# Latent attention's output turned on VectorE in 32 by 32 squares, and the range test summed on GpSimd

## The chip, the cores and the metric

The kernel runs on one core of a Trainium2 chip. The metric is the device time of one execution in microseconds (us); shown are the median of three runs and, for the reading of the profile, one profiled execution. The engines are TensorE (PE, with its weight loads PEld), VectorE (DVE), ScalarE (ACT), GpSimd (POOL) and SyncE (SP), which here only issues DMAs.

## The reference, cut to what matters

Eight sequences of 1024 tokens and 256 channels, all in fp32, go through two layers with a residual each: first a causal latent attention, then a stack of two local-attention layers, which the change does not touch. The first, on normalised x:

```
c_kv   = x @ W_kv_down                        # 256 -> 128
k_rope = rotary(c_kv @ W_k_rope)              # 32 channels, shared by the heads
k, v   = c_kv @ W_k_up, c_kv @ W_v_up         # 16 heads of 16
q      = x @ W_q                              # 16 heads of 16
q_rope = rotary(x @ W_q_rope)
scores = (q k^T per head + q_rope k_rope^T) / sqrt(48), causal
attn   = softmax(scores) @ v
out    = x + attn @ W_o
```

The part `q_rope k_rope^T` is the same for all 16 heads, so the kernel takes its exponential once for all heads and multiplies: exp(a + b) = exp(a) exp(b).

## The kernel before, in words

The latent attention (`mla`) works through the batches b = 0 to 7, each in 36 steps. A step is a unit of the score matrix: four heads (group g, heads 4g to 4g+3) by 128 keys (block kb) by up to 512 queries (half c; c = 1, the later queries, comes first). Units 0 to 25 are c = 1, 26 to 35 are c = 0. The scores are held with the keys on the partitions.

The order on PE, DVE, ACT and POOL is written out by hand; each engine runs its own queue in order. At step s:

- `scores` (L422, L430): PE makes the scores of unit s into two PSUM tiles `sc`, ACT takes the exponentials into two tiles `pt` of 128 by 1024.
- `turned` (L444): DVE multiplies both `pt` of unit s-1 by the rotary exponentials `er`, which lie in SBUF as `pt` does.
- `values` (L455): PE multiplies the `pt` of unit s-2 by the values into `acc`, which has 32 rows for each of the four heads: 16 of output, then a row of ones' products, the softmax's denominator (VW = 17 columns for each head in `v`). When a group of heads is complete for a half, ACT copies `acc` to `oaT` (512 columns, queries along the free axis).
- then the tasks that a table puts beside the step (`at(step, who, name, ...)`, who = -1, 0, 1, 2 being the batch before, this one and the next two), and one finished group.

The tasks that matter here:

- `rotary` (L400, L401, L403): PE makes one block `psR` of the rotary scores in a PSUM bank, ACT takes the exponential into `er` and adds each row up in `most` (an accumulator, which is a read instruction of its own on ACT), DVE takes the row's minimum into `least`, and POOL clears the triangle above the diagonal in the blocks that have one. The eight blocks of c = 1 are made at steps 27 to 34 for the next batch, the four of c = 0 at steps 11 to 15 for the batch itself; for batch 0 the blocks of c = 1 are made in a row before step 0. `most` and `least` are tested at the end against TURN = 1e17 and 1/TURN; their verdict decides with others whether an exact path, not run here, has to replace the result.
- `value` (L76): v = c_kv @ W_v_up, copied from PSUM by DVE.
- `finished`: four transpositions on PE (`flip`, L203) turn a group's `oaT` to 128 queries by four heads in PSUM (`pst`); DVE takes the reciprocal of the denominators (L472, `rs`) and multiplies (L473) into `onat`.
- `out_turn` (L203, L78): for two blocks of 128 queries, four more transpositions on PE turn `onat` back to channels by queries (`pso`), and ACT copies them to `oT`.
- `out_add` (L200, L500, L501): PE multiplies `oT` by `wout` (W_o), DVE adds x, and SP stores the result to DRAM (`x2d`).

PSUM banks for these tasks come from a pool of two (`bank`, L203's and L200's outputs alike). A matrix product with weights (`times`) is cut in four instructions of 32 output rows each. In the last batch the tail's tasks are held back and run after the last step; the local layers follow, their weights being loaded meanwhile.

Of the kernel before, what the change touches and what calls it, by code (L numbers as in the profile page):

```python
# [29 lines left out]
F32 = mybir.dt.float32  # L30
AF = mybir.ActivationFunctionType
ALU = mybir.AluOpType
# [49 lines left out]
def preln_mla_local_kernel(  # L82
# [72 lines left out]
    def mla(ctx: ExitStack, verdict):  # L155
# [42 lines left out]
        def times(out, w, rhs, start, stop):  # L198
            for four in QUARTER:
                nc.tensor.matmul(out[four], w[:, four], rhs, start=start, stop=stop)  # L200

        def flip(out, t):
            nc.tensor.transpose(out, t, ident)  # L203
# [13 lines left out]
        nc.sync.dma_start(wknat, W_k_up)  # L217
        wv = wp.tile([P, D], F32, name="wv")
        nc.sync.dma_start(wv, W_v_up)
        wout = late.tile([P, 2, D], F32, name="wout")  # L220
        nc.sync.dma_start(wout, W_o.rearrange("(c p) d -> p c d", p=P))

# [34 lines left out]

        ers = [late.tile([P, 1280 + 2048 * c], F32, name=f"er{c}") for c in range(2)]  # L260

        most = wp.tile([P, B * 12], F32, name="most")
        least = wp.tile([P, B * 12], F32, name="least")

        class Batch:

# [128 lines left out]
            def rotary(self, c, kb):  # L395
                q0, w, er = self.block(c, kb)
                ps = bank(f"psR{self.b}_{c}_{kb}")
                times(ps[:, :w], self.rk[:, kb * P : (kb + 1) * P], self.rq[:, q0 : q0 + w], True, True)
                n = 12 * self.b + 8 * (1 - c) + kb
                nc.scalar.activation(er, ps[:, :w], AF.Exp, scale=SCALE, accum_out=most[:, n : n + 1])  # L400
                nc.vector.tensor_reduce(least[:, n : n + 1], er, AX.X, ALU.min)  # L401
                if q0 == kb * P:
                    nc.gpsimd.affine_select(  # L403
                        out=er[:, :P], in_=er[:, :P], pattern=[[1, P]],
                        compare_op=ALU.is_ge, fill=0.0, base=0, channel_multiplier=-1,
                    )

            def start(self):
                b = self.b
                self.onat = late.tile([P, NT, NH, HD], F32, tag="onat", name=f"onat{b}")  # L410
                self.rs = small.tile([P, NT, NH], F32, tag="rs", name=f"rs{b}")
                self.acc = {}

            def scores(self, key, parts):

# [49 lines left out]
                return ended  # L465

            def finished(self, c, g, oT):
                ps = bank(f"pst{self.b}_{c}_{g}").rearrange("p (i h d) -> p i h d", i=4, h=4)
                for i in range(4):
                    flip(ps[:, i].rearrange("p h d -> p (h d)"), oT[:, i * P : (i + 1) * P])  # L470
                r = self.rs[:, 4 * c : 4 * c + 4, 4 * g : 4 * g + 4]
                nc.vector.reciprocal(r, ps[:, :, :, HD])  # L472
                nc.vector.tensor_tensor(  # L473
                    self.onat[:, 4 * c : 4 * c + 4, 4 * g : 4 * g + 4, :], ps[:, :, :, :HD],
                    r.unsqueeze(3).to_broadcast([P, 4, 4, HD]), ALU.mult,
                )

            def out_turn(self, t):
                if t == 4:
                    self.oTs, self.adds = {}, {}  # L480
                elif t == 0:
                    verdict(self.rs.rearrange("p t h -> p (t h)"), f"a{self.b}")
                ps = bank(f"pso{self.b}_{t}").rearrange("p (i q) -> p i q", i=4)
                for i in range(4):
                    flat = self.onat[:, t + i // 2].rearrange("p h d -> p (h d)")
                    flip(ps[:, i, :], flat[:, (i % 2) * P : (i % 2 + 1) * P])
                self.oTs[t] = late.tile([P, 4, P], F32, tag="oT", name=f"oT{self.b}_{t}", bufs=2)
                on_a(self.oTs[t], ps)

            def out_add(self, t, i, c=None):  # L490

                if i == 0 and not c:
                    self.adds[t] = bank(f"psx{self.b}_{t}").rearrange("p (i d) -> p i d", i=2)
                ps = self.adds[t]
                for n in range(2) if c is None else (c,):
                    times(ps[:, i], self.oTs[t][:, 2 * i + n, :], wout[:, n, :], n == 0, n == 1)
                if i == 1 and c != 0:
                    del self.oTs[t], self.adds[t]
# [11 lines left out]
        for step, who, *what in (  # L510
# [5 lines left out]
            (5, 0, "query", 0, 0, 1), (5, -1, "out_turn", 0), (5, 1, "normalise", 0, 1),  # L516
            (6, -1, "out_add", 0, 0), (6, -1, "out_turn", 2), (6, 1, "normalise", 1, 0),
# [23 lines left out]
            (30, 1, "rotary", 1, 3), (30, 0, "out_turn", 4),  # L541
# [3 lines left out]
            (34, 1, "rotary", 1, 5), (34, 0, "out_turn", 6), (34, 2, "statistics", 1, 0),  # L545
            (35, 0, "out_add", 6, 0), (35, 0, "out_add", 6, 1, 0),
        ):
            at(step, who, *what)
# [28 lines left out]
        line, done = [], []  # L577
        with tc.manual_schedule(engines={E.PE, E.DVE, E.Activation, E.Pool}):
            for b in range(B + 1):
                for step in range(len(units) if b < B else 9):  # L580
                    if b == B - 1 and step == ALONE:
                        banks.close()
                        third = banks.enter_context(tc.tile_pool(name="pscore2", bufs=1, space=PSUM))
                        shared = itertools.cycle((pscore, pscore, third))
                    if b < B:
                        if step == 0:
                            batches[b].start()
                        line.append((batches[b], units[step], batches[b].scores(step, units[step])))
                    if len(line) > 1 or b == B:
                        for bt, unit, pts in line[-2 : -1] if b < B else line[-1:] if step == 0 else []:  # L590
                            bt.turned(unit, pts)
                    if b == B and step == 0:
                        for act, args in held[:3]:
                            act(*args)
                    ended = []
                    if len(line) > 2 or b == B and line:
                        bt, unit, pts = line.pop(0)
                        ended = [(bt, e) for e in bt.values(unit, pts)]
                    if b == B and step == 0:
                        for act, args in held[3:]:  # L600
                            act(*args)
                    do(b, step)
                    if done:
                        bt, e = done.pop(0)
                        bt.finished(*e)
                    done += ended

        ok = small.tile([P, 2, B * 12], F32, tag="okr", name="okr", bufs=1)
        nc.vector.tensor_scalar(ok[:, 0, :], most, TURN, None, ALU.is_le)
        nc.vector.tensor_scalar(ok[:, 1, :], least, 1 / TURN, None, ALU.is_ge)  # L610
        verdict.add(ok.rearrange("p m n -> p (m n)"), "turn")


    ST = CH // P
# [1155 lines left out]
```

## Time and profile before

| | |
|---|---|
| median of 3 runs | 3413.71 us (3412.76 to 3415.95) |
| profiled execution | 3414.97 us, span 3413.2 us |
| latent attention | up to about 1030 us of the span |
| from one batch's stores of x2d to the next's | 123.02 us |
| PE, DVE, ACT, POOL busy in one such period (274.00 to 397.02 us) | 122.0, 108.2, 91.8, 9.7 us |
| granted PE clock in it | 1.00 |

How to read the profile's groups: line, engine, operation, output and inputs with their shapes, the number of instructions, then busy us and the mean ns of one, then the engine's idle time just before them and what ended it. Instructions of one engine overlap a little at their ends, so the distance from start to start is somewhat shorter than the mean duration (for two L444 in a row 2.27 us, for one 1.22). In a timeline a row has the start, the length of a run of instructions from first start to last end, and their number. POOL's spans are rough.

### The profile page before, as it was taken

What the parts mean: (1) busy time and instruction counts of PE and PEld (TensorE: products, weight loads), DVE (VectorE), ACT (ScalarE), POOL (GpSimd) and SP (SyncE); (2) the same over time, 40 slices, a digit from 0 to 9 for tenths busy, and PEclk for the clock granted to TensorE, in tenths of its full rate; (3) what the DMA queues carried; (4) which work ended last, traced back from release to release, by engine and by line L of the source; (5) the groups of instructions that cost most, each with busy time, mean ns of one, the idle gap of its engine ahead of it and who ended that gap; (6) DMA issues with size and microseconds to landing.
All of it is one profiled execution on the core that took longest, in us unless ns stands there. A gap on an engine that the chain in (4) does not pass through costs nothing.

```text
span 3413.2 us, 80002 instructions
## 1 busy us (share of the span) xinstructions
PE 3344.6 (98%) x34690; PEld 1847.4 (54%) x34690; DVE 2585.4 (76%) x3785; ACT 1702.7 (50%) x2106; POOL 1344.3 (39%) x1031
## 2 busy tenths in 40 slices
PE   8999999999997899999999999999999999999999
PEld 2434333443434565666566666566666666666665
DVE  6888988988887777777767776667777767777763
ACT  5777777777762344444444344444344444344441
POOL 1000000000006655555555555555555555545540
PEclk9999999999999999999999999999999999999999
DMA  1000000000032333233232333334243233333231
GB/s 62 8 20 26 8 20 26 11 20 11 14 110 83 86 87 94 78 106 88 78 99 82 90 95 106 99 96 118 83 118 94 85 108 86 102 108 91 82 94 45
DMA packets 203575, 248.82 MB, mean 73 GB/s; under 512 B 23455, under 2 KB 171342, under 8 KB 203086
## 3 DMA queue, kind: packets, MB, share of 16 engines
q1 hardware_dynamic: 201230, 241.21, 24.3%
q8 instruction: 274, 4.49, 0.6%
q10 hardware_dynamic: 1984, 2.41, 0.2%
q14 instruction: 87, 0.71, 0.1%
HBM read 134.50 MB, written 109.05 MB: 71 GB/s over the span
## 4 chain that ended last, share of the span: by engine, by line
PE 87%; DVE 7%; ACT 2%; issue 2%; POOL 1%; DMA 1%; SPq 0%; ACTq 0%; DVEq 0%
PE ag L1024 16%; PE pair L824 12%; PE sc L422 9%; PE acc L455 8%; PE psy L1059 7%; PE psw L969 7%; PE pv L851 6%; PE o L936 5%; PE pair L895 4%; PE psR L200 2%; PE psq L200 2%; PE psx L200 2%; PE s L944 1%; DVE turned L863 1%; DVE rs L948 1%
## 5 line engine op out<-in xcount | busy, mean ns | idle before, releaser
L444 DVE TENSOR_TENSOR pt<-pt,er 128x1024 f32<-128x1024 f32 x576 | 676.6, 1223 | 6.7 <-ACT pt L430 5.6
L430 ACT ACTIVATE pt<-sc 128x1024 f32<-128x1024 f32 x576 | 559.4, 1024 | 231.5 <-PE sc L422 209.4
L1024 PE MATMUL ag<-d,l 128*128 128x512 f32 x1408 | 640.6, 597 | 1.3 <-ACT ge L1032 0.8
L838 POOL TENSOR_TENSOR t<-t,t 128x1024 f32<-128x1024 f32 x128 | 301.9, 2358 | 756.0 <-DVE t L834 756.0
L824 PE MATMUL pair<-l_qkv,xT 128*128 128x512 f32 x1024 | 469.1, 601 | 3.0 <-ACT pt L901 1.0
L1024 PEld LDWEIGHTS ag<-d,l 128*128 128x128 f32 x1408 | 262.2, 190 | 310.0 <-issue 276.7
L901 ACT ACT_TABLE_LOAD x120 | 154.0, 1283 | 547.8 <-PE pair L895 547.7
L125 POOL TENSOR_TENSOR rn<-ss,half 128x16 f32<-128x16 f32 x128 | 372.9, 2913 | 13.8
L422 PE MATMUL sc<-q,k 32*128 32x512 f32 (+3 forms) x3072 | 347.7, 524 | 4.7 <-ACT pt L430 4.6
L831 DVE TENSOR_TENSOR t<-pair,l_cos 128x1024 f32<-128x1024 f32 x128 | 156.4, 1222 | 245.8 <-ACT sq L829 241.1
L824 PEld LDWEIGHTS pair<-l_qkv,xT 128*128 128x128 f32 x1024 | 190.5, 192 | 238.4 <-issue 207.1
L455 PE MATMUL acc<-pt,v 128*32 128x512 f32 (+3 forms) x3072 | 316.2, 498 | 0.1
L829 ACT ACTIVATE sq<-pair 128x1024 f32<-128x1024 f32 x128 | 131.1, 1024 | 303.4 <-issue 234.4
L1059 PE MATMUL psy<-l,hid 128*128 128x256 f32 x1280 | 281.5, 379 | 0.0
L1033 DVE SCALAR_TENSOR_TENSOR hid<-ag,l_b,ge 128x512 f32<-128x512 f32 x160 | 116.0, 725 | 206.8 <-ACT ge L1032 178.9
L1059 PEld LDWEIGHTS psy<-l,hid 128*128 128x128 f32 x1280 | 243.2, 190 | 46.7 <-issue 15.3
L901 ACT ACTIVATE pt<-pair 128x1024 f32<-128x1024 f32 (+1 forms) x256 | 235.0, 968 | 57.7 <-PE pair L895 56.4
L403 POOL TENSOR_SCALAR_AFFINE_SELECT er<-er 128x128 f32<-128x128 f32 x64 | 47.2, 737 | 530.0 <-DVE least L401 530.0
L844 POOL TENSOR_TENSOR t<-t,rn 128x1024 f32<-128x1024 f32 x128 | 243.4, 1902 | 10.0
L936 PEld LDWEIGHTS o<-pt,v 128*32 128x32 f32 x7680 | 201.4, 110 | 77.5 <-issue 70.8
L936 PE MATMUL o<-pt,v 128*32 128x128 f32 x7680 | 237.4, 274 | 3.4 <-POOL pt L903 3.2
L851 PE MATMUL pv<-l_qkv,xT 128*128 128x512 f32 x512 | 240.6, 592 | 0.0
(131 smaller groups left out, 4851.3 us busy)
## 6 DMA issues: line engine op xcount, KB each, us to landing
z<-turned SPq DMA_DIRECT2D x512, 128.0 KB
qkT<-z SPq DMA_DIRECT2D x128, 512.0 KB
y<-xs SPq DMA_DIRECT2D x128, 128.0 KB
h<-y SPq DMA_DIRECT2D x32, 512.0 KB
x<-in_L_attn_x_dram SPq DMA_DIRECT2D x16, 512.0 KB
x2d<-x SPq DMA_DIRECT2D x32, 256.0 KB
xs<-x2d SPq DMA_DIRECT2D x16, 512.0 KB
x<-x2d SPq DMA_DIRECT2D x16, 512.0 KB
```

The lines of the kernel that those rows point to most:

```text
L125: nc.gpsimd.tensor_tensor(out_, in_, half[:, :n], ALU.pow)
L422: nc.tensor.matmul(two[n // 2][:, n % 2, lo : lo + w], self.k[g][rows, kb * P : (kb + 1) * P], self.q[rows, g // 2, q0 : q0 + w], start=Tr ...
L430: nc.scalar.activation(pt, sc, AF.Exp, scale=SCALE)
L444: nc.vector.tensor_tensor(t, t, er.to_broadcast([P, 1024 // w, w]), ALU.mult)
L455: nc.tensor.matmul(self.acc[g][32 * n : 32 * n + 32, q0 - c * 512 :], self.v[:, kb, h * VW : h * VW + 32], pts[n // 2][:, n % 2, lo : lo + w],
L824: nc.tensor.matmul(qk[:, n].rearrange("p h d -> p (h d)"), self.left(i)[c], w["qkv"][:, c, n * INNER : (n + 1) * INNER], start=(c == 0), s ...
L838: nc.gpsimd.tensor_tensor(t1, t1, t2, ALU.add)
L851: nc.tensor.matmul(pv, self.left(i)[c], self.w["qkv"][:, c, 2 * INNER :], start=(c == 0), stop=(c == 1))
L901: nc.scalar.activation(pt[:, :, : n * P], flat[:, :, : n * P], AF.Exp, scale=-1.0)
L936: nc.tensor.matmul(o[32 * j : 32 * j + 32, g, a, :], vs[m][:, h * DH + a * 32 : h * DH + a * 32 + 32], pts[m][g][:, place(j), off : off + ...
L1024: nc.tensor.matmul(ps, w["1"][:, c, i, :], d[:, c, :], start=(c == 0), stop=(c == 1))
L1059: nc.tensor.matmul(ps[:, t, :], hid[:, i, cols], w["2"][:, i, :], start=(t == i == 0), stop=False)
```

## The change

- `finished` no longer uses PE. DVE transposes `oaT` itself, which it does within squares of 32 by 32: each head's 32 rows by 512 queries become 16 squares with 32 queries on the partitions (`nat`). Reciprocal and product follow, now from SBUF; the results of two groups (e = 0, 1) lie side by side in one tile, so that its squares are 32 wide.
- `out_turn` goes. In its place `turn_back`, one step after the second group of a pair is finished, transposes that tile once more on DVE, which gives `oT` directly: 512 queries, and the channels of eight heads on the partitions, in another order than before (head 4 (2m + e) + r has partitions 32 r + 16 e and on). The rows of `wout` are loaded in the same order, by eight DMAs instead of one.
- The copy of v from PSUM moves from DVE to ACT.
- The range test: no row sums and no minima. ACT takes a second exponential of each rotary block, with the sign reversed (`inverse`, one buffer of 128 by 512), and POOL adds both `er` and `inverse` into one tile of running sums (`ends`). At the end its maximum is compared with TURN. POOL's clearing of the triangle comes after the adds.

```diff
-        nc.sync.dma_start(wout, W_o.rearrange("(c p) d -> p c d", p=P))
+        for e in range(2):
+            for r in range(4):
+                lo = 32 * r + HD * e
+                nc.sync.dma_start(
+                    wout[lo : lo + HD],
+                    W_o.rearrange("(m e r p) d -> e r p m d", m=2, e=2, r=4)[e, r],
+                )
...
-                on_v(
+                on_a(
                     self.v[:, 2 * g : 2 * g + 2, : NH * VW].rearrange("p a (h d) -> p a h d", h=NH)[..., :HD],
...
-                nc.scalar.activation(er, ps[:, :w], AF.Exp, scale=SCALE, accum_out=most[:, n : n + 1])
-                nc.vector.tensor_reduce(least[:, n : n + 1], er, AX.X, ALU.min)
+                nc.scalar.activation(er, ps[:, :w], AF.Exp, scale=SCALE)
+                inverse = wp.tile([P, 512], F32, tag="inverse", name=f"inverse{self.b}_{c}_{kb}")
+                nc.scalar.activation(inverse[:, :w], ps[:, :w], AF.Exp, scale=-SCALE)
+                for what in (er, inverse[:, :w]):
+                    nc.gpsimd.tensor_tensor(ends[:, :w], ends[:, :w], what, ALU.add)
...
             def finished(self, c, g, oT):
-                ps = bank(f"pst{self.b}_{c}_{g}").rearrange("p (i h d) -> p i h d", i=4, h=4)
-                for i in range(4):
-                    flip(ps[:, i].rearrange("p h d -> p (h d)"), oT[:, i * P : (i + 1) * P])
...
+                nat = late.tile([P, 16, 32], F32, tag="onat", name=f"onat{self.b}_{c}_{g}", bufs=3)
+                nc.vector.transpose(nat.rearrange("p b d -> p (b d)"), oT)
+                r = self.rs[:, c, g]
+                nc.vector.reciprocal(r, nat[:, :, HD])
+                e = g % 2
+                if e == 0:
+                    self.onat[c, g // 2] = nat
                 nc.vector.tensor_tensor(
...
+                    self.onat[c, g // 2][:, :, HD * e : HD * e + HD], nat[:, :, :HD],
+                    r.unsqueeze(2).to_broadcast([P, 16, HD]), ALU.mult,
+                )
+
+            def turn_back(self, c, g):
+                if g % 2:
+                    t = late.tile([P, 512], F32, tag="oT", name=f"oT{self.b}_{c}_{g}", bufs=3)
+                    nc.vector.transpose(t, self.onat.pop((c, g // 2)).rearrange("p b d -> p (b d)"))
+                    self.oTs[c, g // 2] = t
...
+        nc.vector.tensor_reduce(ok, ends, AX.X, ALU.max)
+        nc.vector.tensor_scalar(ok, ok, TURN, None, ALU.is_le)
```

In the table of tasks the four `out_turn` entries go and nothing else moves; in the main loop `turn_back` stands before `finished`, one step behind it.

More of the change, by code (lines that the diff above doesn't have):

```diff
@@ L260, in mla @@
         ers = [late.tile([P, 1280 + 2048 * c], F32, name=f"er{c}") for c in range(2)]
-        most = wp.tile([P, B * 12], F32, name="most")
-        least = wp.tile([P, B * 12], F32, name="least")
+        ends = wp.tile([P, 512], F32, name="ends")
+        nc.gpsimd.memset(ends, 0.0)
         class Batch:
@@ L398, in rotary @@
                 times(ps[:, :w], self.rk[:, kb * P : (kb + 1) * P], self.rq[:, q0 : q0 + w], True, True)
-                n = 12 * self.b + 8 * (1 - c) + kb
-                nc.scalar.activation(er, ps[:, :w], AF.Exp, scale=SCALE, accum_out=most[:, n : n + 1])
-                nc.vector.tensor_reduce(least[:, n : n + 1], er, AX.X, ALU.min)
+                nc.scalar.activation(er, ps[:, :w], AF.Exp, scale=SCALE)
[3 more added lines that the diff above has]
+                    nc.gpsimd.tensor_tensor(ends[:, :w], ends[:, :w], what, ALU.add)
                 if q0 == kb * P:
@@ L409, in start @@
                 b = self.b
-                self.onat = late.tile([P, NT, NH, HD], F32, tag="onat", name=f"onat{b}")
-                self.rs = small.tile([P, NT, NH], F32, tag="rs", name=f"rs{b}")
-                self.acc = {}
+                self.rs = small.tile([P, 2, 4, 16], F32, tag="rs", name=f"rs{b}")
+                self.acc, self.onat, self.oTs, self.adds = {}, {}, {}, {}
             def scores(self, key, parts):
@@ L467, in finished @@
             def finished(self, c, g, oT):
-                ps = bank(f"pst{self.b}_{c}_{g}").rearrange("p (i h d) -> p i h d", i=4, h=4)
-                for i in range(4):
-                    flip(ps[:, i].rearrange("p h d -> p (h d)"), oT[:, i * P : (i + 1) * P])
-                r = self.rs[:, 4 * c : 4 * c + 4, 4 * g : 4 * g + 4]
-                nc.vector.reciprocal(r, ps[:, :, :, HD])
+                nat = late.tile([P, 16, 32], F32, tag="onat", name=f"onat{self.b}_{c}_{g}", bufs=3)
[5 more added lines that the diff above has]
+                    self.onat[c, g // 2] = nat
                 nc.vector.tensor_tensor(
-                    self.onat[:, 4 * c : 4 * c + 4, 4 * g : 4 * g + 4, :], ps[:, :, :, :HD],
-                    r.unsqueeze(3).to_broadcast([P, 4, 4, HD]), ALU.mult,
-                )
[L478 to L488, printed above, removed]
+                    self.onat[c, g // 2][:, :, HD * e : HD * e + HD], nat[:, :, :HD],
+                    r.unsqueeze(2).to_broadcast([P, 16, HD]), ALU.mult,
+                )
+            def turn_back(self, c, g):
[3 more added lines that the diff above has]
+                    self.oTs[c, g // 2] = t
+                if (c, g) == (0, 3):
+                    verdict(self.rs.rearrange("p c g b -> p (c g b)"), f"a{self.b}")
             def out_add(self, t, i, c=None):
@@ L495, in out_add @@
                 for n in range(2) if c is None else (c,):
-                    times(ps[:, i], self.oTs[t][:, 2 * i + n, :], wout[:, n, :], n == 0, n == 1)
+                    col = (t + i) % 4 * P
+                    times(ps[:, i], self.oTs[t // 4, n][:, col : col + P], wout[:, n, :], n == 0, n == 1)
                 if i == 1 and c != 0:
-                    del self.oTs[t], self.adds[t]
+                    del self.adds[t]
                     two = slice(t, t + 2)
@@ L515, in mla @@
             (4, 0, "keys", 1, 1, 1), (4, 0, "query", 0, 0, 0), (4, 1, "normalise", 0, 0),
-            (5, 0, "query", 0, 0, 1), (5, -1, "out_turn", 0), (5, 1, "normalise", 0, 1),
-            (6, -1, "out_add", 0, 0), (6, -1, "out_turn", 2), (6, 1, "normalise", 1, 0),
+            (5, 0, "query", 0, 0, 1), (5, 1, "normalise", 0, 1),
+            (6, -1, "out_add", 0, 0), (6, 1, "normalise", 1, 0),
             (7, -1, "out_add", 0, 1), (7, -1, "out_add", 2, 0, 0),
@@ L540, in mla @@
             (29, 1, "rotary", 1, 2), (29, 1, "rotary", 1, 7),
-            (30, 1, "rotary", 1, 3), (30, 0, "out_turn", 4),
+            (30, 1, "rotary", 1, 3),
             (31, 1, "rotary", 1, 6), (31, 0, "out_add", 4, 0),
@@ L544, in mla @@
             (33, 1, "rotary", 1, 4),
-            (34, 1, "rotary", 1, 5), (34, 0, "out_turn", 6), (34, 2, "statistics", 1, 0),
+            (34, 1, "rotary", 1, 5), (34, 2, "statistics", 1, 0),
             (35, 0, "out_add", 6, 0), (35, 0, "out_add", 6, 1, 0),
@@ L576, in mla @@
         E = mybir.EngineType
-        line, done = [], []
+        line, done, turning = [], [], []
         with tc.manual_schedule(engines={E.PE, E.DVE, E.Activation, E.Pool}):
@@ L592, in mla @@
                     if b == B and step == 0:
-                        for act, args in held[:3]:
+                        for act, args in held[:2]:
                             act(*args)
@@ L599, in mla @@
                     if b == B and step == 0:
-                        for act, args in held[3:]:
+                        for act, args in held[2:]:
                             act(*args)
                     do(b, step)
+                    if turning:
+                        bt, e = turning.pop(0)
+                        bt.turn_back(*e)
                     if done:
@@ L605, in mla @@
                         bt.finished(*e)
+                        turning.append((bt, e[:2]))
                     done += ended
[L608 to L611, printed above, removed]
+        ok = small.tile([P, 1], F32, tag="okr", name="okr", bufs=1)
+        nc.vector.tensor_reduce(ok, ends, AX.X, ALU.max)
+        nc.vector.tensor_scalar(ok, ok, TURN, None, ALU.is_le)
+        verdict.add(ok, "turn")
     ST = CH // P
```

## The prediction

> **What bounds the kernel now.** First the page: busy shares, then the chain.
>
> ```profile
> PE 3344.6 (98%) x34690; PEld 1847.4 (54%) x34690; DVE 2585.4 (76%) x3785; ACT 1702.7 (50%) x2106; POOL 1344.3 (39%) x1031
> ...
> PE 87%; DVE 7%; ACT 2%; issue 2%; POOL 1%; DMA 1%; SPq 0%; ACTq 0%; DVEq 0%
> ```
>
> TensorE carries 87% of the chain. The change touches only the latent attention, about the first 1030 us, so next the engines in one of its periods: the stores of x2d start at 150.98, 274.00 and 397.02 us, so a batch takes 123.02 us.
>
> ```profile
> 274.00:397.02 123.02, 122.01 (x1352) 49.37 (x1348) 108.24 (x142) 91.79 (x126) 9.70 (x10) 1.00 0.06 19
> ```
>
> The columns are PE, PEld, DVE, ACT and POOL, busy us (and instructions). PE is the bound at 122.0 of 123.0; DVE has 14.8 us left per batch, ACT 31, POOL nearly all. Then the groups by form, for what is taken from PE and DVE:
>
> ```profile
> L203 PE MATMUL pst<-ident,oaT 128*128 128x128 f32 x256 | 42.0, 287 | 3.5 <-ACT er L400 3.4 <-ACT oaT L78 0.2
> ...
> L203 PE MATMUL pso<-ident,onat 128*128 128x128 f32 x128 | 21.1, 286 | 0.7 <-DVE onat L473 0.7
> ...
> L863 DVE STREAM_TRANSPOSE turned<-t 128x512 f32<-128x512 f32 x28 | 18.1, 682 | 4.0 <-POOL t L844 4.0
> ```
>
> Last the timelines of DVE and POOL where both work, because the change gives POOL much to do:
>
> ```profile
> 387.79 2.44 DVE L444 TENSOR_TENSOR pt<-pt,er 128x1024 f32<-128x1024 f32 x2
> ...
> 387.94 1.21 POOL L403 TENSOR_SCALAR_AFFINE_SELECT er<-er 128x128 f32<-128x128 f32 x1 [9.43 <-DVE least L401]
> ```
>
> ```profile
> 2476.80 1.96 DVE L1077 TENSOR_TENSOR x<-xs,x 128x512 f32<-128x512 f32 x1
> ...
> 2476.31 1.90 POOL L844 TENSOR_TENSOR t<-t,rn 128x1024 f32<-128x1024 f32 x1
> ```
>
> The select normally takes 0.29 us; begun inside a product `pt*er`, it takes 1.21, ending just after the first of the two products. The other way round, L1077 (0.69 us alone) was begun inside a POOL product and took 1.96: it ended 0.55 us after POOL did. The two engines exclude each other, a whole instruction at a time.
>
> [...] the trace's nearest row (L838, 1024 columns) is 2358 ns, 2.30 ns a column[...]
>
> **The change part by part.**
>
> *PE, removed.* 64 `pst` and 32 `pso` sets of four flips. In the PE timeline the next matmul starts 0.585 us after a set starts (276.36 to 276.95), so 96 x 0.585 = 56.2 us. At step 15 the second set waits 0.48 us for a PSUM bank; with it gone, 8 x 0.48 = 3.8. Together **-60 us**: a batch asks PE for 115.5 us.
>
> *DVE.* Out: the 96 minima, 48 x 0.682 + 16 x (0.550 + 0.418 + 0.278) = 52.7, and 32 copies of v at 0.692 = 22.1. In: 96 transpositions like L863 at 0.682 = 65.5. Reciprocal and product by rs are as many as before (249, 424 ns; now from SBUF, not shown, taken alike; the width is the same, so either way under 0.1 us each). Net -9 us, 108.2 to 107.0 a batch. By itself this hides behind PE: adding DVE's work less PE's over the steps, DVE falls at most 3.7 us behind (step 3, where a finished group, turn_back and statistics meet). It may be some 4 us late: the values of a step are asked for two steps later, about 7.5 us after its scores start, and are ready at the earliest after 3.5.
>
> *ACT.* Out: 96 accumulator reads (20.1) and 32 copies of oT (18.8). In: 96 second exponentials, priced as the first (29.2 + 8.1 + 6.4 + 4.4 = 48.1), 32 copies of v at 0.60 (as oaT). Net +28 us, 3.5 a batch against 31 idle; free while spread. But the pool of `inverse` has one buffer: each second exponential waits until POOL has added the one before, and behind it in ACT's queue stand the next exponentials of the scores.
>
> *POOL.* 192 adds. A batch has 6x512 + 2x(384 + 256 + 128) = 4608 columns twice: 9216 x 2.30 ns = 21.2 us, 170 in all. Idle time for it exists; the price is the lock.
>
> *The lock, batches' next blocks.* In steps 27 to 34 eight blocks of the next batch are made (seven times in the run). PE took 27.9 us for these steps, and without six flip sets asks 24.4. [...] 8 pairs of `pt*er` at 2.27 (start to start) = 18.2, four products by rs = 1.4, adds 6656 columns x 2.30 = 15.3, selects about 0.8: 35.7, or 11.3 too much. The transpositions and reciprocals (5 us) lie beside POOL's adds. [...] 11.3 + 1.5 less 4 of slack leaves 9 us. Followed step by step, the wait for `inverse` comes on top at step 29, where two blocks fall together, and steps 1 to 3 cannot win back what DVE lags: I take 11 us a time. Lower end 5 (more lies beside transpositions, or DVE's pipelining lets less through), upper 15 (nothing lies beside, and the ACT wait compounds). 7 x 11 = **+77 us**.
>
> *The batch's own blocks*, steps 11 to 15: 2560 columns, 5.9 us of adds, with some room around. At step 12 `psn` waits for the bank that the second exponential still reads, and that waits for POOL: some 1.1 us more than the 0.53 it waits now, and up to 1 us of lock at 14. I take 2, range 0.5 to 3: 8 x 2 = **+16**.
>
> *Start.* In the first batch the eight blocks are made in a row from 35 us on. POOL's chain of 16 adds lasts 16.5 us with the selects; the last `inverse` can start after 14 of them, near 50 us, and the exponentials of step 1, which started at 45.5, come behind it: **+5**, range 3 to 8.
>
> *Elsewhere.* wout in eight DMAs instead of one puts some 3 us (7 issues at about 0.45) before the load of batch 1 on SP; its statistics ended at 16.0 us and DVE was next needed at 23.6, so nothing; without that cover, 3. The final test (one reduction for two compares) waits for POOL's last add; about 0 to 2 us where weights of the next stage are fetched, as the stall there (DVE waits for l_fcos until 966.9) moves with it: 0, within 5 either way.
>
> Sum: -60 + 77 + 16 + 5 = +38. Against the profiled execution, 3414.97 (span 3413.2): 3453. The median of the runs is 1.3 lower: **3452**.
>
> **Rivals.**
> *Faster: the lock costs little.* If POOL's adds fall mostly where DVE idles or works from PSUM, there remain -60, +5, and the `inverse` wait at step 29 (1.3 us, 7 times) and perhaps 4: -42, **3372**. For it: DVE has 14.8 us idle a batch, and turned, reciprocals and PSUM reads are another 19. Against it: eight blocks come within eight steps in which DVE has hardly any idle time. It decides at (60 - 5 - 16)/7 = 5.6 us of stall per stretch: below that the kernel is faster. Chance 0.15.
> *No change, the two cancel*, 5 to 6.5 us a stretch: about **3414**. Chance 0.06.
> *Worse: nothing overlaps and ACT's wait for `inverse` feeds back*, 15 us a stretch and 3 beside the own blocks: -60 + 105 + 24 + 8 = +77, **3491**. For it: POOL is held up by DVE as well, so the buffer comes free a product later. Chance 0.2.
> *DVE the bound without the lock*: its 107.0 against 115.5 speaks against it; the margin of 0.3 us at step 3 would cost 1 or 2 us a batch. In the ranges.
>
> **How the numbers follow.** The main case, +20 to +60, has 0.59; with the worse one, slower by over 0.2% (7 us, about what a measurement of this kernel can tell) 0.79; within it 0.06; faster 0.15. The lower ends, -60 + 35 + 4 + 3, give 3396; I set the low end at 3400, which leaves out the faster rival, and the high one at 3500, a little over the worse.
>
> **What would show it.** In the profile after: no pst and pso on PE, 96 transpositions on DVE near 0.68 us; POOL's adds well over 1.2 us on average; `pt*er` well over 1.22 us on average in steps 27 to 34, with `acc` waiting for `pt` on PE there; the stores of x2d about 128 us apart instead of 123. It is wrong if pt*er stays at 1.22 and the period falls below 119 (the faster rival), or if PE's waits there are for ACT and not for DVE's products.

## The result, and the profile after

The changed kernel takes **3500.32 us** (median of 4 runs, 3494.84 to 3501.35), the kernel before 3413.68 beside it (3412.76 to 3415.95): ratio 1.0252, 95% interval 1.0240 to 1.0264, slower by 86.6 us. The profiled execution took 3501.2 us (span 3499.5). Forecast were 3452 and a range up to 3500.

The page: busy time by engine, then the engines' shares of the chain that ended last.

```profile
PE 3371.4 (96%) x34306; PEld 1838.2 (53%) x34306; DVE 2650.6 (76%) x3753; ACT 1734.1 (50%) x2106; POOL 1621.0 (46%) x1224
...
PE 78%; DVE 12%; POOL 4%; ACT 3%; issue 2%; DMA 1%; SPq 0%; ACTq 0%; DVEq 0%; POOLq 0%
```

PE has 384 instructions fewer, the 96 flip sets of four, and yet 27 us more busy time. Its share of the chain fell from 87% to 78%, and DVE and POOL took what it lost. Stores of x2d now start at 304.56, 437.80 and 570.98 us, 133.2 apart instead of 123.02. One such period; the columns are PE, PEld, DVE, ACT and POOL (busy us, instructions), the granted PE clock, the DMA share and GB/s:

```profile
437.80:570.98 133.18, 125.35 (x1304) 48.81 (x1298) 116.59 (x138) 95.74 (x126) 44.60 (x34) 0.96 0.05 17
```

PE is idle for 7.8 us of it (1.0 before), and its clock, 1.00 before, is 0.96. What PE waited for in this period (total, times, longest):

```profile
PE sc L430 <- ACT pt L438: 3.9, 1, 3.9
PE psn L203 <- ACT inverse L408: 2.0, 1, 2.0
PE acc L463 <- DVE pt L452: 1.3, 2, 0.7
PE psR L200 <- ACT inverse L408: 0.5, 1, 0.5
```

In the same period of the kernel before there were two waits of 0.5 us. The one of 3.9 us, in the timelines of PE, ACT, POOL and DVE around the two blocks of step 29:

```profile
560.52 2.99 PE L430 MATMUL sc<-q,k 32*128 32x512 f32 x8 [3.94 <-ACT pt L438]
563.44 1.93 PE L463 MATMUL acc<-pt,v 128*32 128x384 f32 x16
...
554.86 0.60 ACT L408 ACTIVATE inverse<-psR 128x512 f32<-128x512 f32 x1 [1.52 <-POOL ends L410]
555.36 0.27 ACT L406 ACTIVATE er<-psR 128x128 f32<-128x128 f32 x1
559.27 0.28 ACT L408 ACTIVATE inverse<-psR 128x128 f32<-128x128 f32 x1 [3.65 <-POOL ends L410]
559.45 1.93 ACT L438 ACTIVATE pt<-sc 128x1024 f32<-128x1024 f32 x2
...
554.91 2.13 POOL L410 TENSOR_TENSOR ends<-ends,er 128x512 f32<-128x512 f32 x1
557.12 2.12 POOL L410 TENSOR_TENSOR ends<-ends,inverse 128x512 f32<-128x512 f32 x1
...
549.18 4.50 DVE L452 TENSOR_TENSOR pt<-pt,er 128x1024 f32<-128x1024 f32 x2
...
554.24 3.88 DVE L452 TENSOR_TENSOR pt<-pt,er 128x1024 f32<-128x1024 f32 x2
```

Read it upwards. A pair of DVE's products takes 4.50 or 3.88 us instead of 2.35, because the products take turns with POOL's adds (e7 and e8 test this below). POOL's adds take 2.12, and 1.26 to 1.34 alone, for the same reason. The small `inverse` of 128 columns waits 3.65 us until POOL has read the one buffer, and behind it in ACT's queue stand the exponentials of the next scores, whose bank PE needs. Then a surprise: the eight matmuls after the pause take 2.99 us, where eight of the same shape take 1.14 at 567.19. The granted clock beside them (window, its length, PE busy and so on, the clock third from the end):

```profile
557.00:560.50 3.50, 0.00 (x0) 0.00 (x0) 1.12 (x2) 1.23 (x3) 3.27 (x5) 0.87 0.00 0
560.50:563.50 3.00, 2.98 (x12) 1.07 (x16) 2.36 (x2) 2.72 (x4) 1.54 (x2) 0.50 0.00 0
563.50:566.00 2.50, 2.50 (x27) 1.12 (x28) 2.30 (x2) 1.64 (x3) 2.42 (x2) 0.50 0.00 0
```

At a clock of 0.50 eight matmuls of this shape take 2.09 us at 495.79 us of the change and at 962.27 of the kernel before. The rest fits the second of the two `sc` tiles, which ACT has read only at 561.4 us (559.45 + 1.93); no run parts the two.

The whole lengthening, 86.3 us of span, divides by the stores into 20.2 ahead of the first, 50.6 in the five periods after it, 17.8 over the last two batches, and -2.3 after.

### The profile page after: what moved, and what is told of

It is laid out like the page before. It is cut to its first block, busy times and chain, and to the rows that moved or that the text cites. A ratio compares the mean times of both kernels' runs of the same rounds, so it can differ in the third digit from the quotient of the medians.

```text
span 3499.5 us, 79439 instructions
## 1 busy us (share of the span) xinstructions
PE 3371.4 (96%) x34306; PEld 1838.2 (53%) x34306; DVE 2650.6 (76%) x3753; ACT 1734.1 (50%) x2106; POOL 1621.0 (46%) x1224
## 4 chain that ended last, share of the span: by engine, by line
PE 78%; DVE 12%; POOL 4%; ACT 3%; issue 2%; DMA 1%; SPq 0%; ACTq 0%; DVEq 0%; POOLq 0%
PE ag L1037 16%; PE pair L837 12%; PE sc L430 7%; PE psy L1072 6%; PE psw L982 6%; PE acc L463 6%; PE pv L864 5%; PE o L949 5%; PE pair L908 3%; POOL ends L410 3%; DVE pt L452 3%; PE psq L200 2%; PE psx L200 1%; DVE turned L876 1%; PE s L957 1%
## 5 line engine op out<-in xcount | busy, mean ns | idle before, releaser
L452 DVE TENSOR_TENSOR pt<-pt,er 128x1024 f32<-128x1024 f32 x576 | 741.8, 1335 | 99.7 <-ACT pt L438 99.5
L430 PE MATMUL sc<-q,k 32*128 32x512 f32 (+3 forms) x3072 | 385.0, 539 | 34.1 <-ACT pt L438 34.1
L463 PE MATMUL acc<-pt,v 128*32 128x512 f32 (+3 forms) x3072 | 347.8, 510 | 13.7 <-DVE pt L452 12.9
L844 DVE TENSOR_TENSOR t<-pair,l_cos 128x1024 f32<-128x1024 f32 x128 | 156.4, 1222 | 244.3 <-ACT sq L842 244.1
L410 POOL TENSOR_TENSOR ends<-ends,er 128x512 f32<-128x512 f32 (+1 forms) x96 | 144.6, 1506 | 380.7 <-ACT er L406 378.6
L430 PEld LDWEIGHTS sc<-q,k 32*128 32x128 f32 x3072 | 163.9, 187 | 229.2 <-ACT pt L438 171.8
L842 ACT ACTIVATE sq<-pair 128x1024 f32<-128x1024 f32 x128 | 131.1, 1024 | 302.2 <-issue 237.1
L1072 PEld LDWEIGHTS psy<-l,hid 128*128 128x128 f32 x1280 | 243.2, 190 | 46.7 <-issue 15.3
```

The source lines that it names most:

```text
L430: nc.tensor.matmul(two[n // 2][:, n % 2, lo : lo + w], self.k[g][rows, kb * P : (kb + 1) * P], self.q[rows, g // 2, q0 : q0 + w], start=Tr ...
L452: nc.vector.tensor_tensor(t, t, er.to_broadcast([P, 1024 // w, w]), ALU.mult)
L463: nc.tensor.matmul(self.acc[g][32 * n : 32 * n + 32, q0 - c * 512 :], self.v[:, kb, h * VW : h * VW + 32], pts[n // 2][:, n % 2, lo : lo + w],
L1072: nc.tensor.matmul(ps[:, t, :], hid[:, i, cols], w["2"][:, i, :], start=(t == i == 0), stop=False)
```

## The experiments

Each was run beside the kernel before on one chip: e1 to e4, e5 to e8 and e9 to e12 on three different ones, where the kernel before takes 3413.5, 3413.7 and 3413.4 us. So the chip is not what parts the medians of different groups. "Period" is the distance between stores of x2d in the profiled execution.

| kernel | median us | ratio to before (95%) | period us |
|---|---|---|---|
| before | 3413.5 | 1 | 123.02 |
| after | 3500.32 | 1.0252 (1.0240 to 1.0264) | 133.2 |
| e1 er added twice | 3445.15 | 1.0091 (1.0075 to 1.0108) | 126.46 |
| e2 no adds | 3398.33 | 0.9953 (0.9936 to 0.9969) | 120.27 |
| e3 turning alone | 3430.88 | 1.0048 (1.0031 to 1.0065) | 125.10 |
| e4 test alone | 3523.40 | 1.0318 (1.0301 to 1.0335) | 136.6 |
| e5 turning, no test | 3390.96 | 0.9929 (0.9913 to 0.9946) | 119.36 |
| e6 and no turning back | 3380.79 | 0.9898 (0.9881 to 0.9914) | 118.21 |
| e7 writes only | 3398.29 | 0.9949 (0.9933 to 0.9966) | 120.28 |
| e8 more inverse buffers | 3451.16 | 1.0106 (1.0089 to 1.0123) | 126.47 |
| e9 no turning | not read, see there | | 117.27 |
| e10 test on ACT | 3403.83 | 0.9972 (0.9960 to 0.9983) | 121.21 |
| e11 and spaced | 3401.91 | 0.9966 (0.9952 to 0.9979) | 121.06 |
| e12 and v divided | 3401.41 | 0.9965 (0.9951 to 0.9979) | 121.10 |

### The halves of the change, and its adds

The first four take the change apart. The theories that the expectations name are spelled out in them, A here and L beside e7: A is the prediction's account, that the loss comes from POOL's adds and `pt*er` excluding each other, as the select (1.21 us instead of 0.29) and L1077 (1.96 instead of 0.69) did in the kernel before; the others are its rivals.

**e1**, the whole change, but nothing reads `inverse`:

```diff
-                for what in (er, inverse[:, :w]):
+                for what in (er, er):
                     nc.gpsimd.tensor_tensor(ends[:, :w], ends[:, :w], what, ALU.add)
```

> The changed kernel, but POOL adds er twice and never inverse: as many adds of the same size on POOL, but no second exponential waits for POOL (left out: the lower half of the range test). Theory A [...]: most of the loss stays, the stretch of steps 27 to 34 still stalls by about 9 us, the period is 125 to 128 us and the time 3420 to 3450. Theory B (the loss is ACT's queue, held by the single buffer of inverse, and the slow PE clock after the pauses that this makes): the period falls to 116 to 119 us, the time to 3355 to 3385. Theory C (the transpositions on VectorE are the cost): hardly changed, above 3480.

**e2**, without the two adds (both exponentials stay):

```diff
-                for what in (er, inverse[:, :w]):
-                    nc.gpsimd.tensor_tensor(ends[:, :w], ends[:, :w], what, ALU.add)
```

> The changed kernel without POOL's adds (left out: the range test's sums; both exponentials on ACT stay, with nobody waiting for inverse). Theories A and B: -60 us for the flips and at most some 10 of waits by a VectorE at 107 of 115.5 us a batch: 3355 to 3370, period 115.5 to 117. Theory C: above 3414.

**e3**, the transpositions and the copies of v on ACT as in the change, with the accumulators and the minima of the kernel before:

```diff
-                nc.scalar.activation(er, ps[:, :w], AF.Exp, scale=SCALE)
-                inverse = wp.tile([P, 512], F32, tag="inverse", ...
-                nc.scalar.activation(inverse[:, :w], ps[:, :w], AF.Exp, scale=-SCALE)
-                for what in (er, inverse[:, :w]):
-                    nc.gpsimd.tensor_tensor(ends[:, :w], ends[:, :w], what, ALU.add)
+                n = 12 * self.b + 8 * (1 - c) + kb
+                nc.scalar.activation(er, ps[:, :w], AF.Exp, scale=SCALE, accum_out=most[:, n : n + 1])
+                nc.vector.tensor_reduce(least[:, n : n + 1], er, AX.X, ALU.min)
```

> The transpositions on VectorE and v's copy on ACT as in the changed kernel, the range test as before (ACT's accumulator, VectorE's minimum, no second exponential). VectorE then asks 107.0 + 6.6 = 113.6 us a batch against PE's 115.5. Theories A and B: 3360 to 3395, with waits for VectorE in the steps that make blocks. Theory C: above 3414.

**e4**, the kernel before, with the change's range test and nothing else of it:

```diff
-                n = 12 * self.b + 8 * (1 - c) + kb
-                nc.scalar.activation(er, ps[:, :w], AF.Exp, scale=SCALE, accum_out=most[:, n : n + 1])
-                nc.vector.tensor_reduce(least[:, n : n + 1], er, AX.X, ALU.min)
+                nc.scalar.activation(er, ps[:, :w], AF.Exp, scale=SCALE)
+                inverse = wp.tile([P, 512], F32, tag="inverse", ...
+                nc.scalar.activation(inverse[:, :w], ps[:, :w], AF.Exp, scale=-SCALE)
+                for what in (er, inverse[:, :w]):
+                    nc.gpsimd.tensor_tensor(ends[:, :w], ends[:, :w], what, ALU.add)
```

> The kernel before, with the range test by sums on POOL and the second exponential, one buffer of inverse; transpositions on PE as before. Theory A: 8 steps with 18 us of products, 15 of adds and 27.9 of PE: a stall of 4 to 8 us in seven stretches, 3450 to 3480. Theory B: ACT's queue is held as long as in the changed kernel, 3470 to 3510, with PE at half its clock after the pauses. Theory C: 3407 to 3421, no change.

*Measured.* e1 3445, e2 3398, e3 3431, e4 3523. The range test by sums by itself costs 110 us, more than the whole change; the turning makes it less bad. From e2 to the change it costs 102.0, and of that 55.2 go when ACT no longer waits for POOL (the change less e1) and 46.8 more when POOL adds nothing (e1 less e2). So the adds are dear, as forecast, in two parts of like size. The miss is the other end: **e2, with no add at all, is only 15 us faster than before, where 43 to 58 were expected**, and e3 is 17 slower where 19 to 54 faster were expected. e2 lies between the ranges of A and B and that of C. e3 lies where theory C has it, which takes the transpositions for the cost; e1 and e4 rule C out for the whole change, but not for this part. e4, at 3523, lies above every range named for it. The -60 of PE did not come.

In e4 PE waits for the same thing at several places, since its flips take banks in turn with the rotary blocks:

```profile
PE pso L203 <- ACT inverse L401: 3.0, 1, 3.0
PE pst L203 <- ACT inverse L401: 2.2, 1, 2.2
PE psn L203 <- ACT inverse L401: 2.0, 1, 2.0
```

Its mean clock is 0.981, like the 0.982 of the change; in e1, e2 and e3 it is 0.993 to 0.994.

### What the adds cost: taking turns and the buffer

**e7**, for each block nine fills of a scratch tile in place of the two adds. Theory L: the 46.8 us from e2 to e1 are DVE's products and POOL's reading adds taking turns.

```diff
-                for what in (er, inverse[:, :w]):
-                    nc.gpsimd.tensor_tensor(ends[:, :w], ends[:, :w], what, ALU.add)
+                for _ in range(9):
+                    nc.gpsimd.memset(fill[:, : w // 2], 0.0)
```

> The change with each block's two sums on POOL replaced by nine fills of w/2 columns, which read no SBUF and take about as long; nothing reads inverse, so the minimum and maximum are not tested. ACT never waits for POOL. Theory L [...]: about the run without sums, 3395 to 3410, pt*er 1.22 us. Rival M (a busy POOL costs the time by its instructions, by the late selects behind them, or by its writes): 3430 to 3450.

**e8**, the whole change with more room for `inverse`:

```diff
-                inverse = wp.tile([P, 512], F32, tag="inverse", name=f"inverse{self.b}_{c}_{kb}")
+                inverse = wp.tile(
+                    [P, w if w == P else 512], F32, tag="narrow" if w == P else "inverse",
+                    name=f"inverse{self.b}_{c}_{kb}", bufs=1 if w == P else 2,
+                )
```

> The whole change, but inverse has two buffers of 512 columns and one for the blocks of 128, in place of one (onat has 2 in place of 3), so that ACT's second exponential seldom waits for POOL's sums. Theory A (of the 102 us that the sums cost, some 55 are ACT's wait for the one buffer, with the scores' exponentials behind it and PE's slower clock after its pause): 3440 to 3455, mean clock 0.99, no wait of sc for ACT's pt over 1 us. Rival B (POOL is then the one that is late, or the lock alone makes the pauses): 3475 to 3500.

*Measured.* e7 3398.29, e2 3398.33: a POOL that is busy for 36 us a period instead of 11, but whose fills read nothing, costs nothing, as theory L wanted. The groups of e7 (count, busy us, mean ns):

```profile
L453 DVE TENSOR_TENSOR pt<-pt,er 128x1024 f32<-128x1024 f32 x576 | 675.2, 1218 | 68.6 <-ACT pt L439 68.6
L411 POOL MEMSET fill<- 128x256 f32 x432 | 135.0, 312 | 23.0
```

and those of e8, where POOL reads:

```profile
L455 DVE TENSOR_TENSOR pt<-pt,er 128x1024 f32<-128x1024 f32 x576 | 755.1, 1359 | 57.7 <-ACT pt L441 57.7
L413 POOL TENSOR_TENSOR ends<-ends,er 128x512 f32<-128x512 f32 x48 | 90.9, 1894 | 277.6 <-ACT er L406 276.3
...
L411 ACT ACTIVATE inverse<-psR 128x512 f32<-128x512 f32 x48 | 29.6, 616 | 4.3 <-POOL ends L413 4.3
```

`pt*er` takes 1.22 us on average over the whole of e7, where POOL's fills only write, as in e2, and 1.36 over the whole of e8, where POOL's adds read. So these products take turns with the adds and not with the fills. Rival M is out. Other work of DVE runs beside POOL's at its own length, which the prediction took for granted. In the change the transpositions of `oaT` that lie inside one add take 0.70 us, as those apart from all adds do, and the reciprocals 0.25 either way; one of them:

```profile
104.55 0.70 DVE L479 STREAM_TRANSPOSE onat<-oaT 128x512 f32<-128x512 f32 x1
...
104.18 1.33 POOL L410 TENSOR_TENSOR ends<-ends,er 128x384 f32<-128x384 f32 x1 [7.20 <-ACT er L406]
```

In the kernel before, `oT<-o,rs` (L953), which reads `o` from PSUM, takes 0.67 us inside a product of POOL (L844, 1.90) and 0.67 to 0.68 apart from any.

e8 is 49.2 us faster than the change, as theory A wanted: ACT's exponentials into `inverse` wait 7.6 us in all for POOL instead of 68.4 (blocks of 512: 4.3 instead of 21.7; blocks of 128: none instead of 30.9), the mean clock is 0.994, and in one of its periods no `sc` waits. What PE still waits for there:

```profile
PE acc L466 <- DVE pt L455: 3.9, 5, 1.1
PE psn L203 <- ACT inverse L411: 0.7, 1, 0.7
```

So the 102 us are 49 for the single buffer, the slow clock after its pauses in it, and 53 (e8 less e2) for the turns that products and adds take, with what is left of ACT's wait. e1, where nothing waits for `inverse` to be read, divides them as 55 and 47.

### Where the 60 us of PE went

In e2, with the adds gone, PE is busy nearly all the time and shows only a wait of 0.7 us in a period; its stalls lie inside groups of matmuls and make their rows longer. They are found by the distance from one step's first score matmul to the next's, in the PE timelines. The table has the steps in which e5 to e12 differ, counted from the step in progress at the stores (step 0 here is step 33 of the list of tasks, step 3 its step 0 of the next batch); "less flips" is the kernel before less 0.585 us for each flip set in that step.

```
step  before  less flips   e2    e5    e6    e9    e11
 0     3.52     2.93      3.15  3.15  3.15  3.14  3.15
 1     3.30     2.72      3.00  3.00  3.00  2.73  3.00
 2     3.38     3.38      4.29  4.30  4.29  3.81  3.70
 3     3.36     3.36      3.71  3.71  3.37  3.36  3.80
 8     3.51     2.93      3.90  3.90  3.10  2.92  3.12
 9     3.52     2.93      2.93  2.93  2.98  3.16  4.30
```

From the stores to the start of the step eleven further on, the kernel before takes 37.13 us and e2 36.51, although six flip sets, 3.5 us, went out of it. The windows of that stretch, in the kernel before and in e2:

```profile
397.02:435.49 38.47, 38.47 (x416) 14.74 (x412) 35.98 (x54) 28.63 (x38) 2.43 (x3) 1.00 0.04 16
```

```profile
391.53:430.00 38.47, 38.32 (x394) 14.09 (x390) 38.09 (x57) 28.97 (x36) 3.07 (x3) 1.00 0.05 17
```

DVE, the third pair of numbers, is busy for 38.09 of 38.47 us (35.98 before): in this stretch it is the bound. Its timeline in e2 shows why:

```profile
391.42 0.70 DVE L477 STREAM_TRANSPOSE onat<-oaT 128x512 f32<-128x512 f32 x1
392.15 0.25 DVE L479 RECIPROCAL rs<-onat 128x16 f32<-128x16 f32 x1
392.44 0.42 DVE L483 TENSOR_TENSOR onat<-onat,rs 128x256 f32<-128x256 f32 x1
392.79 2.35 DVE L450 TENSOR_TENSOR pt<-pt,er 128x1024 f32<-128x1024 f32 x2
395.06 0.70 DVE L477 STREAM_TRANSPOSE onat<-oaT 128x512 f32<-128x512 f32 x1
```

From transposition to transposition a step costs DVE 3.64 us, and two of them follow each other, with an addition, statistics and the turning back around them. PE, without its flips, asks 2.93. The flips were taken from the very steps that the transpositions fill.

**e5** leaves out the range test, **e6** the second transposition too, **e9** both transpositions:

```diff
-                inverse = wp.tile([P, 512], F32, tag="inverse", name=f"inverse{self.b}_{c}_{kb}")
-                nc.scalar.activation(inverse[:, :w], ps[:, :w], AF.Exp, scale=-SCALE)
...
-                    t = late.tile([P, 512], F32, tag="oT", name=f"oT{self.b}_{c}_{g}", bufs=3)
-                    nc.vector.transpose(t, self.onat.pop((c, g // 2)).rearrange("p b d -> p (b d)"))
-                    self.oTs[c, g // 2] = t
+                    self.oTs[c, g // 2] = self.onat.pop((c, g // 2)).rearrange("p b d -> p (b d)")
...
-                nc.vector.transpose(nat.rearrange("p b d -> p (b d)"), oT)
+                turned = oT.rearrange("p (b d) -> p b d", d=32)
```

> The change without its range test: no sums on POOL and no second exponential; the test is left out, the transpositions stay. Beside the run without the sums (3398, one batch in 120.27 us) it only takes 48 us from ACT. Theory D (the -60 of PE is lost because DVE has no reserve from the batch's start to step 11, 38.1 us busy of 38.5, and ACT has little in steps 27 to 34, 24.5 of 26.6): only ACT's part comes back, some 1 to 2 us a batch, period 118.5 to 119.5, time 3380 to 3392. Theory P (the second exponentials and the score banks that they hold are what eats it): period 115 to 116.5, time 3355 to 3368. Theory N (PE itself needs the time, its matmuls run slower without the flips between them): no difference, 3395 to 3401.

> As the run without range test, and also without the second of the two transpositions: the normalised values, not turned back, are multiplied by wout, so the attention's output is wrong; DVE has 32 x 0.68 = 22 us less, PE the same work, and the tile onat has 6 buffers in place of 3. Theory D (DVE has no reserve at the batch's start): period 115.5 to 117.5, time 3352 to 3372, at least 15 below the run without range test. Theories P and N: within 4 us of that run.

> As the run without range test (3391), and without either transposition on DVE: reciprocal and product take oT as it lies, so the attention's output is wrong. DVE has 96 x 0.69 = 66 us less, PE the same work. Theory D2 (each finished group costs DVE 1.37 us in a step where PE, without its flips, asks only 2.93 and the products take 2.27; two such steps follow each other, with statistics or an addition beside them; leaving out the second transposition gave back only 10 us because it does not lie in those steps): the period falls to 115.5 to 116.5, time 3355 to 3368. Theory N (PE needs the time by itself): within 5 of the run without the second transposition, 3376 to 3386.

*Measured.* e5 is 7.4 us under e2; theory D's 3380 to 3392 holds, theory P's 3355 to 3368 and theory N's 3395 to 3401 don't. e3 set against e5 shows DVE's want of reserve once more: e3 has the minima in addition, 52.4 us of DVE's time, and 20.3 us of accumulator reads on ACT, and takes 39.9 us more. The reads can't be most of it: e10, below, has twice as many and the second exponentials too, but no minima, and takes 12.9 more than e5. This is why e3 missed. e6 gives 10.2 more for the 22 us that DVE saves: right in direction, but short of the 15 that theory D asked for. In e9 the denominators are no longer where the kernel looks for them, and its verdict on their range sent it on to the exact path after the fast one (15411 us in all); only the stores of the fast path are read. They are 117.27 us apart, and the last group starts at 977.23 us, against 994.95 in e5 and 987.05 in e6. The period falls by 2.1 us, so the transpositions do cost PE time, and step 8 is back at 2.92; theory N, which allowed 5 us beside e6, is out. But theory D2 wanted 115.5 to 116.5, and 1.8 us of the period are still missing. They stand in six steps, 0, 2, 5, 9, 31 and 34, and each time the score matmuls are longer by as much (1.36 to 1.69 us instead of 1.14 to 1.16). These need an `sc` tile that ACT has read, so ACT is taken for the limit there. In e9, around step 31, which took 3.46 us instead of 2.93, the timelines of PE and ACT:

```profile
365.94 1.69 PE L426 MATMUL sc<-q,k 32*128 32x256 f32 x16
```

```profile
366.27 0.64 ACT L78 COPY oaT<-acc 128x512 f32<-128x512 f32 x1
366.74 0.67 ACT L406 ACTIVATE er<-psR 128x512 f32<-128x512 f32 x1
367.27 1.98 ACT L434 ACTIVATE pt<-sc 128x1024 f32<-128x1024 f32 x2
```

The copy of a finished group, an exponential of a rotary block and those of the scores come to 3 us, and the score matmuls, 1.15 us alone, take 1.69. That ACT causes it is read from the timelines; no run took ACT's copy away.

One more place is outside the periods. From the first store of batch 5 to that of batch 7 both the kernel before and e2 take 251.08 us: the gain in the last two batches is nil. Where no next batch lies beside the scores any more, DVE's products run in a row in both; in e2:

```profile
959.78 15.97 DVE L450 TENSOR_TENSOR pt<-pt,er 128x1024 f32<-128x1024 f32 x14
```

and later PE stands 4.0 us at once for DVE's `oT`, where the kernel before waited 2.2 us in three pieces for ACT's. e9 takes 242.54 us there.

### Versions that keep the whole test

**e10** takes both sums with ACT's accumulators, **e11** leaves a step between two finished groups, **e12** also copies half of v on DVE again:

```diff
-                nc.scalar.activation(er, ps[:, :w], AF.Exp, scale=SCALE)
+                nc.scalar.activation(er, ps[:, :w], AF.Exp, scale=SCALE, accum_out=most[:, 0, n : n + 1])
...
-                nc.scalar.activation(inverse[:, :w], ps[:, :w], AF.Exp, scale=-SCALE)
-                for what in (er, inverse[:, :w]):
-                    nc.gpsimd.tensor_tensor(ends[:, :w], ends[:, :w], what, ALU.add)
+                nc.scalar.activation(
+                    inverse[:, :w], ps[:, :w], AF.Exp, scale=-SCALE, accum_out=most[:, 1, n : n + 1]
+                )
...
-                    if done:
+                    rest = bool(done) and not rest
+                    if rest:
                         bt, e = done.pop(0)
...
-                on_a(
+                (on_v if g < 2 else on_a)(
```

> The change with the sums of the range test taken by ACT's accumulators on the two exponentials in place of POOL: the whole test, nothing left out. [...] ACT has 192 accumulator reads, 40 us, more than the run without sums (3398). Theory D2 (ACT has some 2 us left in steps 27 to 34): 3400 to 3410, faster than before by 0.1 to 0.4%. Rival (ACT is the bound in these steps and each read of 0.21 us counts in full there, 8 blocks x 0.42 x 7 = 24 us): 3418 to 3425.

> As the run with the test on ACT, but a step without a finished group is left between two of them: the second of each pair is transposed one step later. Nothing else moves. Theory D2 (two steps of 3.64 us of DVE in a row against 2.93 of PE): 8 to 20 us less than without the space. Rivals (the amount of DVE work in the stretch decides and not its place, or ACT does): within 3 us.

> As the run with the space, and two of the four copies of v of each batch go back from ACT to DVE (those of values 0 and 1, in steps where DVE had 0.6 to 0.7 us of waiting each). If ACT is what is short in steps 27 to 34: 3 to 10 us less than with the space alone. If DVE is: 0 to 8 more.

*Measured.* e10 is 5.5 us over e2 and beats the kernel before, ratio 0.9972 (0.9960 to 0.9983). With the space the median is 1.9 us lower, within the 3 of its rivals and not the 8 to 20 of theory D2: the table shows step 8 down by 0.8 and step 2 by 0.6, and step 9 up by 1.4. So in this stretch it is the amount of DVE's work that decides, not that two such steps are neighbours. Dividing the copies of v makes no difference that these runs can tell. e12's 3401.41, 0.9965 of before (0.9951 to 0.9979), is the fastest that computes everything, and e11 and e10 are not distinguishable from it.

## Why the prediction was wrong

**The step that failed is the first term of the sum, -60**, and with it the sentence on DVE, "By itself this hides behind PE", with its backlog of 3.7 us against some 4 of slack. It measured -15.3 (e2, which has all of the change but the adds). Of the 45 missing, 7.4 are the second exponentials ("free while spread"; e2 less e5), 17.7 are the time of DVE's transpositions (the last group of stores, e5 less e9), and some 20 are left. In e9, which has neither cost, 9 of these lie in the five periods (5 x 1.8, where by the timelines ACT holds up the scores) and 6 to 7 in the last two batches (251.08 - 2 x 7.5 = 236 was due, 242.54 came, with DVE's products in a row); no run parted them further. The balance by batch, 107.0 of DVE against 115.5 of PE, hid a stretch of 38 us without reserve, and the balance by steps allowed a slack that was not there. The flips removed and the transpositions added lie in the same steps, so the two should have been set against each other there: 3.64 against 2.93.

**The costs of the adds, 77 + 16 + 5 = 98, were right: 102.0 measured** (the change less e2). Per period, 11 + 2 = 13 forecast, 133.2 - 120.27 = 12.9 measured. Inside them the shares were off. Some 10 of the 13 were put to products and adds taking turns (the 1.5 us in that sum are what DVE has besides in step 32) and 3 to the wait for `inverse`; it is 6.2 (126.47 - 120.27) and 6.7 (133.2 - 126.47). So the agreement of the sum is in part luck: too much for the turns made up for too little for the wait. The prediction's own sign of error, that PE's waits are for ACT and not for the products, was there: 3.9 us for ACT's `pt` after the blocks of step 29, and 1.3 for the products, which came later, in step 35. Two things made the wait dearer. The small block at step 29 came ahead of the scores' exponentials and behind two long adds, and PE then ran at half clock for 5.5 us. An estimate from the windows: the clock lost in a period is (1 - 0.51) x 2.3 + (1 - 0.81) x 3.0 + 0.5 x 5.5 + 0.04 x 5.0 = 4.6 us, in which PE's work could not go on at its rate; the prediction had no such term, though the kernel before shows such a fall of the clock in its last batches (last section).

**Start.** +5 forecast (3 to 8). The exponentials of step 1 start at 56.25 us instead of 45.54, so +10.7, of which an unknown part is the clock: it was 0.86 over the first 62 us, 1.00 before, and stood at 0.50 from 40.8 to 57.9 us, after a wait of PE for `inverse` of 1.42 us.

**Smaller steps.** POOL's add of 512 columns, taken as 1.18 us from the row of 1024, is 1.26 to 1.34 alone. The transpositions are 0.70 us, the reciprocals and the products by rs, now from SBUF, 0.25 and 0.44 (0.68, 0.25 and 0.42 forecast). The eight DMAs of wout hold SP for 7.88 us, the one before for 0.43, and DVE waits 5.26 us for batch 1's x instead of 1.33; PE's waits beside it are as before (0.67 us twice, before 0.68 twice).

**The rivals.** "Worse", 3491, was the nearest in time, by a mechanism that was half there: ACT's wait for `inverse` feeds back, but products and adds taking turns cost less than forecast, not more. Its nearness is luck: it too counts the whole -60, and makes up for it with 105 + 24 + 8 = 137 for the adds, where 102 came. "Faster" and "cancel" needed under 6.5 us a stretch, 8.5 a period with the batch's own blocks; 12.9 came, so they are out. "DVE the bound without the lock", put at 1 or 2 us a batch, is what happened, with ACT beside it: 120.27 - 115.5 = 4.8 us a batch.

In sum: +38 was -60 + 98, and +87 is -15 + 102.

## What to carry to other kernels

Before an instruction is moved from the bounding engine to one with idle time, set both against each other in the steps where the work lands, with everything that is already there; a balance over a whole batch does not tell that the receiving engine has no reserve in just these steps. A test that only watches the data is better read by an engine that passes over them anyway: here ACT's accumulators took 5.5 us (e10 less e2), and sums on POOL beside `pt*er` 52.8 (e8 less e2). If it must be POOL, a buffer that ACT writes and POOL reads needs a second one, or everything behind ACT's wait pays (49.2 us, the change less e8). Fills on POOL that only write cost nothing here (e7 3398.29, e2 3398.33).

## What was not expected of the hardware

- PE's granted clock fell to a half after a single pause. Two windows of the change after the shorter pause:

```profile
494.70:497.00 2.30, 2.25 (x12) 1.23 (x12) 0.66 (x1) 0.59 (x1) 2.22 (x4) 0.51 0.00 0
497.00:500.00 3.00, 3.00 (x40) 0.90 (x32) 1.03 (x1) 2.09 (x3) 0.26 (x2) 0.81 0.03 5
```

  That is 0.51 for 2.3 us after a pause of 2.04 us, 0.50 for 5.5 us after one of 3.94, and back at 0.96 in the next window. The kernel before does the same in its last batches, so its own trace could have told:

```profile
958.56 1.91 PE L422 MATMUL sc<-q,k 32*128 32x512 f32 x4 [1.21 <-ACT pt L430]
970.43 2.08 PE L422 MATMUL sc<-q,k 32*128 32x512 f32 x4 [3.40 <-ACT pt L430]
```

  Cut into windows of 0.25 us, these stretches have a clock of 1.00 or 0.50 and nothing between, but in the windows of the steps, from whose values their times are worked out. The clock of the change falls at 494.75 us, rises at 498.17, falls at 559.61 and rises at 566.43: 1, 19 and 21 times 3.41 us after the first. In the kernel before it falls at 958.78, rises at 965.61, falls at 969.02 and rises at 975.85: 2, 3 and 5 times 3.41 us after the first. Pauses of 1.21 and 2.04 us were enough for a fall. Two of 0.70 and 0.60 us, shortly after each other in the change (444.4 to 446.3 us), left the clock at 1.00. How much idle time it takes no run shows.
- POOL's own adds were held up too, and not only DVE's products: 1.88 us on average for the adds of `er` with 512 columns (1.86 for `inverse`) against 1.26 to 1.34 alone.
